# A graph attention layer's softmax by matrix products, its table in two parts, and layer 3 run from its last stage

## The chip, the core and the metric

The kernel runs on one core of a Trainium2 chip. The core has five engines, each with its own in-order queue: TensorE (PE; its weight loads are listed apart as PEld), VectorE (DVE), ScalarE (ACT), GpSimd (POOL) and SyncE (SP). SP issues most of the DMAs, POOL the indirect ones and some others. The metric is the time of one execution on the device in microseconds; three runs of the kernel before gave 2410.27, 2411.70 and 2413.79, a median of 2411.7.

## The reference

Four graph layers are applied in turn to x of shape 128 x 64 x 256 (graphs, nodes, features), each as `x = layernorm(x + layer(x))`. Layer 0 is a convolution with four windowed LSTMs, layer 1 a convolution with batch norms, layer 3 a spectral map with the eigenvectors U of the graph's Laplacian (`U (relu(U^T x W1 + b1) W2 + b2)`, per graph). Layer 2, which the change is about, is an attention over 512 edges `src -> dst` with 4 heads:

```
e     = a . leaky_relu(Xq[src] + Xq[dst])   + log(adj[src, dst] + eps)
m     = segment_max(e, src);  ex = exp(e - m[src])
attn  = ex / segment_sum(ex, src)[src]
Y     = segment_sum(attn * Xv[dst], src);   out = Y W_out^T
```

All is in float32.

## The kernel before

X (64 tiles of 128 rows by 256) stays in SBUF. The edges are sorted by source in layer 0 (`sort_edges`, lines 1396 to 1475), and per-edge tables are stored to DRAM as `edge_d` (line 1311) and loaded again for layer 2: `GG` (one-hot of source plus destination, both halves of the partitions), `lg` (logarithms), `kp` (1 where an edge has its predecessor's source), `br` (0 or -1e30 likewise) and `ix` (the row of the attention table for each edge). `attn_d` (line 1313) is that table in DRAM: 64 x 64 rows (destination, source) and 512 rows for edges that are not the last of their pair, 256 floats each; it is zeroed in layer 1 (line 1752).

Layer 2 has three kinds of steps, written as generators and run in an order written out by hand at the end of the kernel; the framework then orders instructions within each engine's queue, by their dependences, near that order.

- `scores` (lines 1908 to 1944), 32 steps of four tiles' worth of rows in two halves of 16 (HU). One step holds two half steps: 4 products with GG (line 1924), ACT's copies out of PSUM (1931), leaky ReLU on DVE (1932), and a half step later 4 products with `az` that sum over features (1878) into two PSUM tiles `sc`, one for each pair of heads. Between them stand the maps of the next step (1901), whose value part goes to DRAM (`xvd`, line 1905, issued by SP).
- the softmax of a half, when its 16 steps are through: `softmax` (1946 to 1964) adds `lg`, takes segment maxima by two scans on DVE, one forward and one backward, subtracts, takes exponentials on ACT, takes segment sums by two more scans, divides and multiplies, for two tiles of 128 x 512 each. `table` (1966 to 1979) transposes the result by PE, lets ACT scatter it into `at` (1974), and has POOL write it into `attn_d` with four indirect DMAs (1977). `fetch` (1981 to 1988) loads the table back as M with eight DMAs of 512 KB, all from SP, each row's 128 columns of 256.
- `values` (2014 to 2031), 33 steps: `load` copies one slice of M by ACT (`mc`, line 1993) and loads xv from DRAM by POOL's queue (1996), one step ahead; `mixed` multiplies (2008) and copies by ACT (`yT`, 2011); then the output product (2029), whose result `Norm` adds to X and normalises in groups of four tiles.

Layer 3 (`blocks`, 2127 to 2134) takes 16 blocks of four tiles through four stages, a software pipeline of 19 steps: `basis` (2096), after which POOL adds a constant `cb` to X (2100), `first_map` (2106), `back` (2114) and `second_map` (2123), with a last layer norm and the store of the block. Its weights are loaded (2066 to 2074) and its constants computed (2079 to 2084) after the scores.

The order: all scores of half 0; then scoring steps with the first softmax between them; table, fetch, scoring steps; seven pairs of scoring and value steps; then value steps, the second softmax and the first layer 3 steps mixed, the second table and fetch; then two value steps to one layer 3 step, and at the end the last layer 3 steps alone.

The functions that the change touches and what calls them:

Of the kernel before, what the change touches and what calls it, by code (L numbers as in the profile page):

```python
# [7 lines left out]
F32 = mybir.dt.float32  # L8
I32 = mybir.dt.int32
# [5 lines left out]
N = 64  # L15
# [1244 lines left out]
def tile_adj_resnorm(ctx: ExitStack, tc: tile.TileContext, I: dict, out: bass.AP, layers: int = 4):  # L1260
# [47 lines left out]
    EDGE = (("GG", E), ("lg", E), ("kp", E + 1), ("br", E + 1), ("ix", 4))  # L1308
# [4 lines left out]
    attn_d = dram.tile([N * N + E, 2 * P], F32, tag="attn_d", name="attn_d")  # L1313

    def edge_tables(t):
        at, o = 0, {}
        for name, w in EDGE:
            o[name] = t[:, at : at + w]
            at += w
        return [o[k] for k in ("GG", "lg", "kp", "br")] + [o["ix"].bitcast(I32)]  # L1320
# [75 lines left out]
    def sort_edges(gk, gp):  # L1396
# [5 lines left out]
        GG, lg, kp, br, ix = edge_tables(edge_s)  # L1402
# [54 lines left out]
        v.memset(kp, 0.0)  # L1457
        v.tensor_tensor(kp[:, 1:E], row[0][:, 1:], row[0][:, : E - 1], ALU.is_equal)
        v.tensor_scalar(br, kp, 1.0, 1e30, ALU.subtract, ALU.mult)
        OS, OD = gt_("kr", [P, E]), gt_("ef", [P, E])  # L1460
        v.tensor_scalar(OS, row[0], pmod, None, ALU.is_equal)
        v.tensor_scalar(OD, row[1], pmod, None, ALU.is_equal)
        v.tensor_tensor(GG, OS, OD, ALU.add)
        ps = gp.tile([P, 512], F32, tag="ps", name="ps")
# [287 lines left out]
    for z in attn_d[: N * N, :].rearrange("(k p a) q -> k p (a q)", p=P, a=4):  # L1752
        nc.sync.dma_start(z, zero)
# [73 lines left out]
    with ExitStack() as l2:  # L1827
# [9 lines left out]
        GG, lg, kp, br, ix = edge_tables(edge_s)  # L1837
# [16 lines left out]
        kf, kb, bf, bb = kp[:, :E], kp[:, 1:], br[:, :E], br[:, 1:]  # L1854
# [6 lines left out]
        es, soft = [[], []], []  # L1861
# [6 lines left out]
        def products():  # L1868
# [12 lines left out]
            if u_ == HU - 1 and c == 1:  # L1881
                next(soft[half])
# [63 lines left out]
        def softmax(half, es):  # L1946

            for c in range(2):
                es.append(sm.tile([P, E], F32, tag="se", name="se"))
                v.tensor_tensor(es[c], sc[half][c], lg, ALU.add)  # L1950
            yield
            for c, e in enumerate(es):
                f = sm.tile([P, 2, E], F32, tag="sf", name="sf", bufs=1)[:, 0, :]
                v.tensor_tensor_scan(f, bf, e, -1e30, ALU.add, ALU.max)
                v.tensor_tensor_scan(f[:, ::-1], bb[:, ::-1], f[:, ::-1], -1e30, ALU.add, ALU.max)
                v.tensor_tensor(e, e, f, ALU.subtract)
                s.activation(e, e, AF.Exp)
                yield
                v.tensor_tensor_scan(f, kf, e, 0.0, ALU.mult, ALU.add)
                v.tensor_tensor_scan(f[:, ::-1], kb[:, ::-1], f[:, ::-1], 0.0, ALU.mult, ALU.max)  # L1960
                yield
                v.reciprocal(f, f)  # L1962
                v.tensor_tensor(e, e, f, ALU.mult)
                yield

        def table(es):

            at = sm.tile([P, 2, E], F32, tag="sf", name="at", bufs=1).rearrange(
                "p a b -> p (a b)").rearrange("p (k b u c i) -> p k b u c i", k=4, b=2, u=HU, c=2)
            for c, e in enumerate(es):  # L1970
                ps = pp.tile([P, 512], F32, tag="m", name="m")
                for k in range(4):
                    te.transpose(ps[:, k * P : (k + 1) * P], e[:, k * P : (k + 1) * P], ident)
                s.copy(at[:, :, :, :, c, :].rearrange("p k b u i -> p (k b) i u"),
                       ps.rearrange("p (k i u) -> p k i u", i=4, u=HU))
            for k in range(4):
                nc.gpsimd.indirect_dma_start(
                    out=attn_d[:, :], out_offset=bass.IndirectOffsetOnAxis(ap=ix[:, k : k + 1], axis=0),
                    in_=at[:, k].rearrange("p b u c i -> p (b u c i)"), in_offset=None)

        def fetch(half):

            M2[half] = lw.tile([P, N, P], F32, tag="M2", name="M2", bufs=2)
            for n0 in range(0, N, 16):
                for b in range(2):
                    nc.sync.dma_start(  # L1986
                        M2[half][b * N : (b + 1) * N, n0 : n0 + 16, :],
                        attn_d[: N * N, b * P : (b + 1) * P].rearrange("(d n) q -> d n q", n=N)[:, n0 : n0 + 16, :])
# [25 lines left out]
        def values():  # L2014
# [3 lines left out]
            for k in range(K + 1):  # L2018
# [6 lines left out]
                if k:  # L2025
                    po = bank() if bank else pp.tile([P, 512], F32, tag="m", name="m")
# [10 lines left out]
        bank = None  # L2037
        sc_, beside[0] = scores(), last_pass()
# [4 lines left out]
        lw, sm = own1(valuing, name="l2w", bufs=1), own1(valuing, name="l2s", bufs=2)  # L2043
        ln = Norm(nc, sm, X, 4, act=True)
        val = values()
        soft += [softmax(h, es[h]) for h in range(2)]
        run(*[sc_] * (HU - NQ + 2))
        for _ in range(3):
            run(sc_, soft[0], soft[0])
        run(soft[0], sc_)  # L2050
        table(es[0])
        run(sc_)
        fetch(0)
        run(*[sc_] * 4)
# [6 lines left out]
        with tc.tile_pool(name="l3w", bufs=1) as l3w, tc.tile_pool(name="l3s", bufs=2) as s3, tc.tile_pool(  # L2061
            name="l3p", bufs=6, space=PSUM
        ) as p3:
            bank = lambda: p3.tile([P, 512], F32, tag="ps", name="ps")
            w1 = l3w.tile([P, 2, P], F32, tag="w31", name="w31")
            nc.sync.dma_start(w1, kio(I["W31"]))
            w2 = l3w.tile([P, D], F32, tag="w32", name="w32")
            nc.sync.dma_start(w2, I["W32"])
            b1 = l3w.tile([P, 1], F32, tag="b31", name="b31")
            nc.sync.dma_start(b1, I["b31"])  # L2070
            nb1 = l3w.tile([P, P], F32, tag="nb1", name="nb1")
            nc.sync.dma_start(nb1, I["b31"].rearrange("p o -> (p o)").partition_broadcast(P))
            cb = l3w.tile([P, D], F32, tag="cb", name="cb")
            nc.sync.dma_start(cb, I["b32"].partition_broadcast(P).rearrange("p o d -> p (o d)"))

            def constants():
                v.tensor_scalar(nb1, nb1, -1.0, None, ALU.mult)
                ps = bank()
                te.matmul(ps[:, :D], b1.to_broadcast([P, P]), w2, start=True, stop=True)
                te.matmul(ps[:, D : D + 1], bdut, ones[:, 0:1], start=True, stop=True)  # L2080
                ru = l3w.tile([P, 1], F32, tag="ru", name="ru")
                v.tensor_copy(ru, ps[:, D : D + 1])
                v.tensor_tensor(cb, cb, ps[:, :D], ALU.add)
                v.tensor_scalar(cb, cb, ru, None, ALU.mult)

# [32 lines left out]
            def second_map(q):  # L2118
                a = uh.pop(q)
                for j in range(0, 4, 2):  # L2120
# [4 lines left out]
                nc.sync.dma_start(ov[:, q * 4 : q * 4 + 4, :], X[:, q * 4 : q * 4 + 4, :])  # L2125

            def blocks():

                NQ = NT // 4
                for q in range(NQ + 3):  # L2130
                    for k, stage in enumerate((basis, first_map, back, second_map)):
# [5 lines left out]
            constants()  # L2137
            run(val, soft[1], val, soft[1], l3, soft[1], val, soft[1], l3, soft[1], val, soft[1], l3)
            table(es[1])
            run(val, l3)  # L2140
            fetch(1)
            run(*[val, val, l3] * 10)
            run(*[val] * 2, *[l3] * (NT // 4))
# [63 lines left out]
```

## Time and profile before

| | us |
|---|---|
| median of three runs | 2411.7 |
| the profiled execution | 2413.07 |
| its span | 2411.2 |
| layers 0 and 1 and the start of layer 2 (to about 1988) | 1988 |
| PE's wait at the first M (2071 to 2083) | 9.7 |
| PE's wait at the second M (2267 to 2276) | 9.4 |
| from PE's last matmul to the end | 12.3 |

The profile shows one execution. Each group of instructions is named by its line in the kernel before, its engine and `out<-in`. "Idle before" is the time in which the engine stood, with the instruction that ended it. A float32 product counts as two matmul records. The granted clock is the share of full speed that TensorE was given.

### The profile page before, as it was taken

What the parts mean: (1) busy time and instruction counts of PE and PEld (TensorE: products, weight loads), DVE (VectorE), ACT (ScalarE), POOL (GpSimd) and SP (SyncE); (2) the same over time, 40 slices, a digit from 0 to 9 for tenths busy, and PEclk for the clock granted to TensorE, in tenths of its full rate; (3) what the DMA queues carried; (4) which work ended last, traced back from release to release, by engine and by line L of the source; (5) the groups of instructions that cost most, each with busy time, mean ns of one, the idle gap of its engine ahead of it and who ended that gap; (6) DMA issues with size and microseconds to landing.
All of it is one profiled execution on the core that took longest, in us unless ns stands there. A gap on an engine that the chain in (4) does not pass through costs nothing. (4 is left out here: it accounts for less than half of the span.)

```text
span 2411.2 us, 29498 instructions
## 1 busy us (share of the span) xinstructions
PE 2289.0 (95%) x9016; PEld 1226.7 (51%) x9016; DVE 1815.5 (75%) x8352; ACT 974.3 (40%) x1750; POOL 76.4 (3%) x115
## 2 busy tenths in 40 slices
PE   7999999999999999999999999998979999898897
PEld 5544654444565544665444644554434433246786
DVE  4666766677887888888888888686967877457577
ACT  2333322242333243332243322333437875456575
POOL 0000000000000000000000000000000000002231
PEclk9999999999999999999999999999989999999899
DMA  6001000000100010100001000012211000511622
GB/s 218 18 18 36 1 35 1 24 30 18 53 1 35 2 52 18 53 35 1 35 36 36 17 18 18 18 49 92 75 45 40 23 23 29 94 40 44 136 89 75
DMA packets 59861, 101.26 MB, mean 42 GB/s; under 512 B 5136, under 2 KB 40080, under 8 KB 59440
## 3 DMA queue, kind: packets, MB, share of 16 engines
q1 hardware_dynamic: 54624, 88.83, 11.6%
q0 software_dynamic: 3216, 10.21, 1.5%
q8 instruction: 72, 1.18, 0.2%
q14 instruction: 93, 0.76, 0.1%
q10 hardware_dynamic: 1856, 0.28, 0.1%
HBM read 67.84 MB, written 31.46 MB: 41 GB/s over the span
## 5 line engine op out<-in xcount | busy, mean ns | idle before, releaser
L1590 PE MATMUL pq<-H,wi 128*128 128x512 f32 (+1 forms) x2016 | 836.4, 547 | 6.1 <-DVE H L1619 4.0
L1596 ACT ACTIVATE gate<-pq,bl 128x512 f32<-128x512 f32 (+1 forms) x504 | 317.6, 635 | 791.0 <-PE pq L1594 642.3
L1590 PEld LDWEIGHTS pq<-H,wi 128*128 128x128 f32 x2016 | 371.9, 191 | 331.0 <-issue 256.7
L1594 PE MATMUL pq<-lh,wh 128*128 128x512 f32 (+1 forms) x1152 | 481.8, 534 | 16.0 <-DVE lh L1614 12.7
L1594 PEld LDWEIGHTS pq<-lh,wh 128*128 128x128 f32 x1152 | 213.1, 190 | 213.3 <-issue 128.3
L1932 DVE SCALAR_TENSOR_TENSOR xs<-xs 128x512 f32<-128x512 f32 x256 | 165.3, 682 | 63.6 <-ACT xs L1931 62.5
L1931 ACT COPY xs<-l 128x512 f32<-128x512 f32 x256 | 136.8, 587 | 74.8 <-PE l L1924 38.6
L1924 PE MATMUL l<-edge_s,xq 64*128 64x512 f32 x512 | 136.0, 629 | 17.5 <-ACT xs L1931 12.5
L1612 ACT ACTIVATE gate<-lc 128x512 f32<-128x512 f32 (+1 forms) x144 | 83.5, 580 | 166.6 <-DVE lc L1608 80.9
L1901 PE MATMUL m<-wqv,xT 128*128 128x512 f32 x256 | 123.0, 617 | 0.8 <-DVE xT L1892 0.8
L1763 PE MATMUL ps<-h,w 128*128 128x512 f32 x256 | 114.9, 608 | 6.9 <-ACT h L1758 6.9
L1745 PE MATMUL ps<-at,w 128*128 128x512 f32 x256 | 116.7, 607 | 3.8 <-ACT at L1741 3.2
L1253 ACT ACTIVATE X<-X,ln_sh,ln_rs 128x256 f32<-128x256 f32 x192 | 99.2, 590 | 19.5 <-DVE ln_sh L1249 13.7
L1237 DVE BATCH_NORM_STATS2 ln_st<-X 128x6 f32<-128x256 f32 x256 | 98.7, 415 | 2.3
L142 DVE COPY AQR<-eps 64x192 f32<-64x192 f32 (+1 forms) x125 | 35.0, 280 | 80.9 <-PE eps L148 80.8
L1901 PEld LDWEIGHTS m<-wqv,xT 128*128 128x128 f32 x256 | 46.0, 192 | 77.1 <-issue 62.5
L1763 PEld LDWEIGHTS ps<-h,w 128*128 128x128 f32 x256 | 49.1, 194 | 67.4 <-issue 57.5
L1924 PEld LDWEIGHTS l<-edge_s,xq 64*128 64x128 f32 x512 | 46.3, 189 | 69.8 <-issue 32.9
L1996 POOL DMA_DIRECT2D xr<-xv x32 | 17.6, 550 | 2007.2 <-DVE xs L1932 1791.2
L1610 DVE TENSOR_TENSOR gate<-gate 128x512 f32<-128x512 f32 (+1 forms) x72 | 43.4, 603 | 45.9 <-ACT gate L1596 45.3
L1745 PEld LDWEIGHTS ps<-at,w 128*128 128x128 f32 x256 | 47.2, 192 | 59.7 <-issue 46.8
L1878 PE MATMUL sc<-xs,az 128*32 128x512 f32 x512 | 68.2, 605 | 3.0 <-DVE xs L1932 3.0
(557 smaller groups left out, 3245.6 us busy)
## 6 DMA issues: line engine op xcount, KB each, us to landing
wi<-in_WihT_dram SPq DMA_DIRECT2D x16, 1024.0 KB, 4.9
wh<-in_WhhT_dram SPq DMA_DIRECT2D x12, 1024.0 KB, 6.9
X<-in_x_dram SPq DMA_DIRECT2D x16, 512.0 KB, 8.9
xd<-X SPq DMA_DIRECT2D x16, 512.0 KB, 2.7
X<-xd SPq DMA_DIRECT2D x16, 512.0 KB, 3.2
xv<-xv SPq DMA_DIRECT2D x32, 256.0 KB, 2.0
xr<-xv POOLq DMA_DIRECT2D x32, 256.0 KB, 3.0
M<-attn_d SPq DMA_DIRECT2D x16, 512.0 KB, 11.2
```

The lines of the kernel that those rows point to most:

```text
L1237: nc.vector.bn_stats(st, self.X[:, k, :])
L1253: nc.scalar.activation(x, x, AF.Identity, bias=sh[:, k : k + 1], scale=rs[:, k : k + 1])
L1590: te.matmul(ps, wi[:, kk, o * P : (o + 1) * P], at(kk, k), start=(kk == 0), stop=(k == 0 and kk == 1))
L1594: te.matmul(ps, wh[:, kk, o * P : (o + 1) * P], hst[:, kk, :M], start=False, stop=(kk == 1))
L1596: s.activation(gates[gt][:, c, :M], ps, AF.Tanh if gt == 2 else AF.Sigmoid, bias=bl[:, p - 1, o : o + 1])
L1612: s.activation(g[2], cs, AF.Tanh)
L1745: te.matmul(ps, w1[:, k, c * P : (c + 1) * P], at[:, k, :], start=(k == 0), stop=(k == 1))
L1763: te.matmul(ps, w2[:, k, c * P : (c + 1) * P], h[:, k, :], start=(k == 0), stop=(k == 3))
L1901: te.matmul(ps, xT[:, i, c, :], wqv[:, c, :], start=(c == 0), stop=(c == 1))
L1924: mms.append(te.matmul(pl[i][:, b, :], xq[i][r, c * P : (c + 1) * P], GG[r, :], start=True, stop=True))
L1931: taken.append(s.copy(x, pl[i][:, b, :]))
L1932: ready.append(v.scalar_tensor_tensor(x, x, 0.2, x, ALU.mult, ALU.max))
```

## The change

The softmax's sums are no longer scans. Two tables are stored with the edges in place of `kp`: `OS`, the one-hot of each edge's source, and `OE`, its transpose in four parts (four PE transposes and one copy in `sort_edges`). After the exponentials the tile is transposed by PE and copied by ACT (`eT`); products with `OE` give the sums per source and row; their maximum with 0.5 is inverted on a 64 x 128 tile; products with `OS` spread the inverses over the edges; and DVE multiplies them with `eT` straight into `at`. `softmax` and `table` are one generator now. The second half's softmax takes each tile's maximum scan as soon as that tile's scores are complete, and stands between value steps alone, with no layer 3 step in it.

The attention table is two tables of 128 columns, so each half is written by four indirect DMAs of its own and read in contiguous runs; `fetch` takes one from SP and one from POOL.

Layer 3's weights and constants come during the scores. Two layer 3 steps stand before the second table's fetch and more right behind it, one to each value step. Within a layer 3 step the stages run from the last to the first. The last block is normalised and stored in two parts of two tiles.

```diff
-    EDGE = (("GG", E), ("lg", E), ("kp", E + 1), ("br", E + 1), ("ix", 4))
+    EDGE = (("GG", E), ("OS", E), ("lg", E), ("br", E + 1), ("OE", 4 * N), ("ix", 4))
...
-    attn_d = dram.tile([N * N + E, 2 * P], F32, tag="attn_d", name="attn_d")
+    attn_d = [dram.tile([N * N + E, P], F32, tag=f"attn_d{b}", name="attn_d") for b in range(2)]
...
+        ps = gp.tile([P, 512], F32, tag="ps", name="ps")
+        for k in range(4):
+            te.transpose(ps[:, k * N : (k + 1) * N], OS[:N, k * P : (k + 1) * P], ident[:N, :N])
+        v.tensor_copy(OE, ps[:, : 4 * N])
...
-    for z in attn_d[: N * N, :].rearrange("(k p a) q -> k p (a q)", p=P, a=4):
-        nc.sync.dma_start(z, zero)
+    for b in range(2):
+        for z in attn_d[b][: N * N, :].rearrange("(k p a) q -> k p (a q)", p=P, a=8):
+            nc.sync.dma_start(z, zero)
...
-            if u_ == HU - 1 and c == 1:
-                next(soft[half])
+            if u_ == HU - 1:
+                run(*[soft[half]] * (2 if half and not c else 1))
...
-        def softmax(half, es):
+        def softmax(half):
...
+            for f, c in ((scored, 0), (shifted, 0), (scored, 1), (shifted, 1)) if half else (
+                    (scored, 0), (scored, 1), (shifted, 0), (shifted, 1)):
+                f(c)
+                yield
+            for e in es:
                 s.activation(e, e, AF.Exp)
-                yield
-                v.tensor_tensor_scan(f, kf, e, 0.0, ALU.mult, ALU.add)
-                v.tensor_tensor_scan(f[:, ::-1], kb[:, ::-1], f[:, ::-1], 0.0, ALU.mult, ALU.max)
-                yield
-                v.reciprocal(f, f)
-                v.tensor_tensor(e, e, f, ALU.mult)
-                yield
+            yield
+            for e in es:
+                ps = scratch()
                 for k in range(4):
                     te.transpose(ps[:, k * P : (k + 1) * P], e[:, k * P : (k + 1) * P], ident)
-                s.copy(at[:, :, :, :, c, :].rearrange("p k b u i -> p (k b) i u"),
-                       ps.rearrange("p (k i u) -> p k i u", i=4, u=HU))
+                eTs.append(sm.tile([P, 4, P], F32, tag="sf", name="eT"))
+                s.copy(eTs[-1].rearrange("p k r -> p (k r)"), ps)
+            yield
+            for eT in eTs:
+                ps = scratch()
+                for k in range(4):
+                    te.matmul(ps[:N, :P], OE[:, k * N : (k + 1) * N], eT[:, k, :], start=(k == 0), stop=(k == 3))
+                rc = sm.tile([N, P], F32, tag="rc", name="rc")
+                v.tensor_scalar(rc, ps[:N, :P], 0.5, None, ALU.max)
+                v.reciprocal(rc, rc)
+                rcs.append(rc)
+            yield
...
+                for k in range(4):
+                    te.matmul(ps[:, k * P : (k + 1) * P], OS[:N, k * P : (k + 1) * P], rc, start=True, stop=True)
+                v.tensor_tensor(at[:, :, :, :, c, :].rearrange("p k b u i -> p (k b) i u"),
+                                eT.rearrange("p k (i u) -> p k i u", u=HU).rearrange("p k (b i) u -> p (k b) i u", b=2),
+                                ps.rearrange("p (k i u) -> p k i u", i=4, u=HU), ALU.mult)
             for k in range(4):
-                nc.gpsimd.indirect_dma_start(
-                    out=attn_d[:, :], out_offset=bass.IndirectOffsetOnAxis(ap=ix[:, k : k + 1], axis=0),
-                    in_=at[:, k].rearrange("p b u c i -> p (b u c i)"), in_offset=None)
+                for b in range(2):
+                    nc.gpsimd.indirect_dma_start(
+                        out=attn_d[b][:, :], out_offset=bass.IndirectOffsetOnAxis(ap=ix[:, k : k + 1], axis=0),
+                        in_=at[:, k, b].rearrange("p u c i -> p (u c i)"), in_offset=None)
...
-            M2[half] = lw.tile([P, N, P], F32, tag="M2", name="M2", bufs=2)
+            M2[half] = lw.tile([P, N, P], F32, tag="M2", name="M2")
             for n0 in range(0, N, 16):
                 for b in range(2):
-                    nc.sync.dma_start(
+                    (nc.sync, nc.gpsimd)[b].dma_start(
                         M2[half][b * N : (b + 1) * N, n0 : n0 + 16, :],
-                        attn_d[: N * N, b * P : (b + 1) * P].rearrange("(d n) q -> d n q", n=N)[:, n0 : n0 + 16, :])
+                        attn_d[b][: N * N, :].rearrange("(d n) q -> d n q", n=N)[:, n0 : n0 + 16, :])
...
-        for _ in range(3):
-            run(sc_, soft[0], soft[0])
-        run(soft[0], sc_)
-        table(es[0])
-        run(sc_)
+        run(*[sc_, soft[0]] * 6)
         fetch(0)
-        run(*[sc_] * 4)
+        run(*[sc_] * 3)
+        constants()
         run(*[sc_, val] * 7)
...
             def second_map(q):
                 a = uh.pop(q)
+                n = 4 if q < NT // 4 - 1 else 2
...
-                nc.sync.dma_start(ov[:, q * 4 : q * 4 + 4, :], X[:, q * 4 : q * 4 + 4, :])
+                    t = q * 4 + j + 2
+                    if t % n == 0:
+                        if n == 2:
+                            ln3.flush()
+                        nc.sync.dma_start(ov[:, t - n : t, :], X[:, t - n : t, :])
...
-                    for k, stage in enumerate((basis, first_map, back, second_map)):
+                    for k, stage in ((3, second_map), (2, back), (1, first_map), (0, basis)):
...
-            run(val, soft[1], val, soft[1], l3, soft[1], val, soft[1], l3, soft[1], val, soft[1], l3)
-            table(es[1])
-            run(val, l3)
+            run(sf, val, sf, val, sf, val, sf, val, sf, l3, l3, val, l3, val)
             fetch(1)
-            run(*[val, val, l3] * 10)
-            run(*[val] * 2, *[l3] * (NT // 4))
+            run(l3, val, l3, val, l3)
+            run(*[val, val, l3] * 8, val, val, *[l3] * (NT // 4))
```

`run` calls each generator it is given once, in order. `scratch` is a PSUM tile: of the pool that layers 2's products use before layer 3's pool is open, of that pool after.

## The prediction

> **What bounds the kernel.** I read the busy table first, then the stretches behind 1980 us, since every large edit is there, then who made TensorE wait, then the queues' timeline. Up to 1988 us PE is the bound and the change hardly touches it. The page's first line and five stretches (us; then busy time and instructions of PE, weight loads, DVE, ACT, POOL; granted clock, DMA share, GB/s):
>
> ```profile
> PE 2289.0 (95%) x9016; PEld 1226.7 (51%) x9016; DVE 1815.5 (75%) x8352; ACT 974.3 (40%) x1750; POOL 76.4 (3%) x115
> ```
> ```profile
> 1988.82:2041.01 52.19, 46.49 (x201) 16.24 (x201) 44.46 (x56) 27.09 (x57) 0.00 (x0) 0.97 0.07 26
> 2055.29:2080.07 24.78, 18.02 (x80) 6.25 (x72) 9.86 (x16) 8.39 (x19) 0.00 (x0) 0.92 1.12 188
> 2190.24:2290.97 100.73, 84.42 (x833) 72.76 (x829) 66.74 (x182) 60.76 (x115) 31.90 (x44) 0.88 0.46 100
> 2290.97:2398.87 107.90, 106.25 (x1024) 94.54 (x1024) 86.81 (x314) 74.42 (x160) 31.03 (x47) 1.00 0.24 77
> 2398.87:2411.20 12.33, 0.01 (x1) 0.00 (x0) 4.57 (x26) 6.31 (x14) 0.00 (x0) 0.70 0.38 128
> ```
>
> PE is full from 2291 to 2399 us, holed before that and idle at the end. In the second row the DMA engines are saturated (share 1.12). PE's waits from 2190 to 2280:
>
> ```profile
> PE m L2008 <- ACT mc L1993: 9.4, 1, 9.4
> PE m L1973 <- DVE se L1963: 3.4, 1, 3.4
> PE ps L2079 <- DVE is_t L1212: 2.3, 1, 2.3
> ```
>
> The first is the wait for the second table M, the second the softmax's division, the third the constants. The timeline around the first half's softmax and table, and the zeroing of the same 4 MB:
>
> ```profile
> 2002.81 3.35 DVE L1962 RECIPROCAL sf<-sf 128x512 f32<-128x512 f32 x1
> ```
> ```profile
> 2055.29 16.05 SPq L1986 DMA_DIRECT2D M<-attn_d  x8
> ```
> ```profile
> 1661.09 7.87 SPq L1753 DMA_DIRECT2D attn_d<-zero  x8
> 2276.40 3.26 PE L2008 MATMUL m<-mc,xr 64*64 64x64 f32 x64 [9.37 <-ACT mc L1993]
> ```
>
> The last line shows what an idle costs afterwards: 64 matmul records in 3.26 us, where undisturbed pairs of 32 take 1.8.
>
> **The change, part by part.** Times are on the clock of before.
>
> **A, first softmax among the scores.** A scoring step is 10.19 us undisturbed (two half steps of 5.1). From the matmuls at 1988.82 to those at 2036.88 stand 8 half steps, 40.8 us; 48.1 were spent, so the softmax cost 7.3, nearly all where DVE held the 3.35 us divisions and two more scans (1.21 each) per column tile in front of the leaky ReLUs. Its transposes cost another 1.0. Removed on DVE per half: 2 x (2 scans 2.4 + 3.35 + 0.68) = 12.9 us. Added on DVE: 2 x (a maximum on 64x128, by L2077 0.2; a division of 128 columns, 3.35/4 = 0.85, bounds 0.15 for four columns and 3.35; a product out of PSUM with scattered writes, 0.68 by L1950 to twice that, since ACT's scattered copy L1974 took 1.0 against 0.53 plain; I take 1.0) = 4.1. Added on PE: two groups of 8 products, each like L2106's 8 (1.79 us), 3.6 in all; bounds 2.0 (by the transposes' 1.0 for 8) and 4.5. PE is the bound here, so that counts in full. What DVE still delays I put at 1.4 (0 to 5): add, two scans and subtraction of the first tile cost 0.1 in the step from 1988.82 to 1999.12, the second tile's follow as closely. After: 1.0 + 3.6 + 1.4 = 6.0 against 8.3: **-2.3** (-5.3 to +2.5).
>
> **B, the wait for the first M.** Before, the transposes (2039.80) stand 5.5 half steps ahead of ACT's first copy out of M (queued in the 46th half step); M landed at 2080.07, PE stood 9.7 us and the step took 21.57 instead of 10.19: 11.4. In the changed order the sums stand after 42 half steps, the products after 44, and ACT's copies after 48. From the products PE has 30.0 us of work (their 1.8, then 5.5 half steps, matmuls of the 50th included) until it needs what lies behind those copies. The chain against it: product and DVE to the first scatter 3.5 (before 3.4); scatters: before 12.1 for four, 2.7 to 3.8 apart, of which POOL's issue is 1.0 and the rest a wait for the one before on the same table. Eight on two alternating tables fit the second issue into that wait, 13.1; bound above, no overlap, 8 x 2.7 = 21.6. Then M: rows of 512 bytes become runs of 8 KB; the nearest row is the zeroing, 4 MB in 4 KB runs, from 1661.09 to 4.9 us after its last issue at 1667.7, 11.5; I take 12, bounds 10 and the old 24.8. Then 3.0 from landing to PE, as at 2080.07 to 2083.10. Sum 31.6, so PE stands 1.6, with a slow stretch after it 2.6 of cost: **-8.8** (-11.4, no wait at all, to +4.6 with M at 24.8; the unoverlapped scatters alone make it -0.3).
> Here a rule speaks against the change: the Trainium skill, "DMA: Bandwidth & Descriptors", section "Issuing engines are not separate DMA queues", says that all queues end on the same 16 engines and a second one saves issue time alone. The saturated row agrees (share 1.12 while SP issued for only 16.05 of 24.78 us). By the rule alone, without the longer runs, M would take 24.8, PE would stand 14.4, and the sum below would be 13.4 us worse here and 5 in C; I follow the zeroing row instead.
> What is queued past: SP stands at M until the scatters are done, with one store of xv behind it (two buffers, so ACT is not held); layer 3's five loads (0.4 us of SP each) come up to the 13th scoring step, 2 us in all on SP, hidden by the scoring steps, whose stores come every 10 us; without that cover they cost their 2. POOL's xr loads wait behind the scatters and four M issues, and are needed only after M anyway.
>
> **C, second softmax, layer 3's start, second M.** From 2190.24 to 2290.97 the PE rows at undisturbed rates add up to 73.9 us (val step 2.73: 0.9 + 1.83; layer 3 block 6.19: 1.78 + 1.79 + 0.89 + 1.73), so 26.8 are waits and slow clock: 16.4 waits, the rest slow stretches such as 3.78 us for 8 products that take 1.79. After: 3.6 more products. The constants (0.8) move into the 51st half step; their 2.3 wait goes. The chain add, scans, subtraction, exponential, transposes, copy, sums, division, product is longer in links and still serial: by DVE's order the second tile's subtraction ends near 2205.5, its exponential 2206.4 (two table loads of 1.28 between), its copy on ACT, behind a layer norm's four (2.08) and another table load, 2212.8, sums 2213.7, products 2216.7 to 2218.5. PE's own work to there is 15.2 behind 2197.8, 2213.0: 5.5 wait, plus 1.5 slow clock. From there to the first matmul that needs the second M lie 42 us of PE work (val steps and layer 3 blocks). Scatters share POOL with eight additions of cb (0.75 each): products + 3.5 + 13 + 6 + landing 11 is about 34: no wait; bounds 0 and 5 (M as slow as before; 14 with scatters unoverlapped too). POOL's M issues stand behind an addition that waits for PE at products + 12.5, before the scatters are through; xr of val steps 15 and 16 stand behind them and are needed at + 39. DVE needs about 7.5 of the 8.9 us that a val step and a block take PE when they alternate one to one; for that coupling 2.0. After: 5.5 + 1.5 + 2.0 + 3.6 = 12.6 against 26.8: **-14.2** (-20 to 0).
>
> **D, the end.** Reversed stages expose the last copy of uh (about 1.1, as at L2123 before) but not two other stalls: 2.7 becomes 1.6. Behind PE's end 12.33 us stand: additions, statistics, eight normalisations in one run (4.02), store 4.4. With the last block normalised and stored in pairs, four remain behind the last statistics: 5.5 + 0.1 + 4.2 = 9.8. Together **-3.6** (-6 to 0).
>
> **E, the edge tables.** Four transposes, a 128x256 copy, 128 KB more to store and load once: **+0.5** (0 to +2). The zeroing has eight issues of 512 KB as before: 0.
>
> Sum: -2.3 - 8.8 - 14.2 - 3.6 + 0.5 = -28.4. The profiled execution took 2413.07 (span 2411.2 and 1.9 around it), 1.4 above the median: 2384.7 on its basis, 2383.3 on the median's. I say 2384.
>
> **Rivals.**
> 1. M is no faster (runs of 8 KB, or scatters that do not overlap). For: issue was not what limited it. Against: the zeroing row. B +13.4, C +5 (landing at 47 against 42): -10.0, 2402.
> 2. The second softmax's links starve PE: ACT's table loads and norms stand in front of each copy twice as long, and the clock falls. For: ACT's chain above already takes 6.4 us from the second exponential to its copy. Against: PE has val steps to fill with. If each link takes twice as long, C +12: -16.4, 2395.
> 3. Slower: POOL generates the four M issues per half so slowly that both M land late. For: SP needed 2.7 us for such an issue; against: POOL's xr issues of 128 rows took 0.55 and a scatter 1.0. At x us each, 4(x - 0.55) comes on B, and what exceeds 8 of it on C; that cancels 28.4 from x = 5.1 on; at 6 it is +7.2, 2419.
> 4. The products cost as much as the divisions did and waits only move: within 0.2% (4.8 us, about what a measurement of this kernel can tell from no change). Against: 3.6 of PE stands for 12.9 of DVE per half.
>
> **How the numbers follow.** Forecast 0.64, rival 1 0.14, rival 2 0.12, rival 3 0.07, rival 4 0.03; rivals 1 and 2 are faster too. Faster 0.90, same 0.03, slower 0.07. The terms' good ends (A -5, B -11, C -20, D -6) leave 2371 if all came together; I take 2372 to 2403, which takes in rivals 1 and 2 and leaves out rival 3.
>
> **What would show it.** A: no 128x512 reciprocal, the two groups of products near 1.8 us, steps behind the 32nd half step near 10.2 but for three of 11 to 12. B: M landing about 12 us after the last scatter, PE waiting under 4 us there. C: no wait for the second M, one hole of 5 us before the transposes. D: under 10 us behind the last matmul. Wrong if M's landings stay near 25 us, if POOL's M issues exceed 5 us, or if layer 3's blocks among the val steps stall.

## The result

The changed kernel takes 2421.9 us (2417.2 to 2426.3) against 2411.7: the ratio is 1.0038, interval 1.0020 to 1.0055. It is slower, by 0.4%, where 2384 was forecast and 2403 was the range's upper end. Its profiled execution is the fastest of its five: 2417.21 us, span 2415.4. Where its slower executions spend their 5 to 9 us more was not profiled; all that follows is about this one, 4.2 us longer in span than the profiled one of before.

Marks that both kernels have locate the difference. These are the X transposes that PE does for each scoring step (line 1890 before, 1896 after), the last product of the value steps (2029, 2055), and the end:

| mark | before, us | after, us | difference, us | gained or lost since the mark above |
|---|---|---|---|---|
| first transposes of the scores | 1807.18 | 1803.90 | -3.3 | -3.3 |
| 17th (before the first softmax) | 1978.01 | 1974.17 | -3.8 | -0.6 |
| 25th (softmax and products done) | 2067.83 | 2061.44 | -6.4 | -2.6 |
| 29th (M there, values begun) | 2120.98 | 2118.11 | -2.9 | +3.5 |
| last value product | 2372.87 | 2380.33 | +7.5 | +10.3 |
| end of the span | 2411.2 | 2415.4 | +4.2 | -3.3 |

The first 3.8 us say little of the change: in the twelve kernels below the first of these transposes began anywhere from 1803.1 to 1813.5 us, with all but the same work ahead of it.

The first line of the changed kernel's profile, then stretches that answer to those shown of before: the first softmax among the scores, the first M from its first issue to ACT's first copy, from the last scores to the first regular triple (two value steps and one layer 3 step), seven triples, and the end behind PE. The columns are as before: us, then busy time and instructions of PE, weight loads, DVE, ACT, POOL; granted clock, DMA share, GB/s.

```profile
PE 2292.2 (95%) x9084; PEld 1233.0 (51%) x9084; DVE 1798.8 (74%) x8355; ACT 969.7 (40%) x1751; POOL 86.3 (4%) x131
```
```profile
1984.98:2037.17 52.19, 50.63 (x223) 18.17 (x224) 36.20 (x53) 30.62 (x64) 0.00 (x0) 1.00 0.07 26
2068.53:2089.78 21.25, 13.42 (x58) 4.38 (x56) 5.86 (x9) 4.48 (x10) 2.15 (x4) 0.89 0.89 213
2187.37:2275.59 88.22, 80.12 (x788) 68.45 (x784) 58.31 (x177) 55.66 (x108) 33.04 (x48) 0.96 0.39 105
2275.59:2373.40 97.81, 85.66 (x883) 76.23 (x883) 60.84 (x225) 60.02 (x130) 25.28 (x40) 0.98 0.22 71
2407.18:2415.40 8.22, 0.00 (x0) 0.00 (x0) 3.38 (x20) 3.27 (x8) 0.00 (x0) 0.50 0.38 128
```

PE does 50.63 us of work in the softmax's stretch where it did 46.49, and the end behind PE is 8.22 us long and not 12.33: those parts do what was forecast. But M takes 21.25 us, and where PE used to be full it is busy for 85.66 of 97.81 us. PE's waits from the last scores on, and the timeline around the first M (SP, POOL, ACT, PE):

```profile
PE m L2034 <- ACT yT L2037: 17.7, 10, 3.5
PE ps L2148 <- ACT uh L2140: 2.9, 1, 2.9
PE ps L2055 <- ACT yT L2037: 2.3, 1, 2.3
```
```profile
2068.53 2.39 SPq L2012 DMA_DIRECT2D M<-attn_d  x4
...
2070.06 2.15 POOL L2012 DMA_DIRECT2D M<-attn_d  x4 [1.55 <-DMA attn_d<-at,edge_s]
...
2089.78 2.01 ACT L2019 COPY mc<-M 128x512 f32<-128x512 f32 x2 [13.46 <-DMA M<-attn_d]
...
2092.38 1.12 PE L1896 MATMUL m<-ident,X 128*128 128x128 f32 x4 [10.41 <-ACT xv L1910]
```

The wait for the second M that led the list of before (9.4 us at once) has given way to ten waits for `yT`. Seven of them are the 1.7 us of the regular triples below. The two longest, 3.55 and 1.82, come where the second M lands, when ACT's first copy out of it had waited 2.5 us. At the first M, ACT stands 13.46 us at its copy, and PE 10.41 us for a copy of `xv` that is queued behind that one on ACT.

A triple in the changed kernel, on PE and on ACT:

```profile
2289.56 0.98 PE L2034 MATMUL m<-mc,xr 64*64 64x64 f32 x32
...
2292.39 0.68 PE L2034 MATMUL m<-mc,xr 64*64 64x64 f32 x16
2294.81 0.68 PE L2034 MATMUL m<-mc,xr 64*64 64x64 f32 x16 [1.74 <-ACT yT L2037]
...
2303.54 0.98 PE L2034 MATMUL m<-mc,xr 64*64 64x64 f32 x32
```
```profile
2291.35 0.37 ACT L2037 COPY yT<-m 128x256 f32<-128x256 f32 x1
2292.43 2.08 ACT L1253 ACTIVATE X<-X,ln_sh,ln_rs 128x256 f32<-128x256 f32 x4 [0.71 <-DVE ln_sh L1249]
2294.41 0.35 ACT L2037 COPY yT<-m 128x256 f32<-128x256 f32 x1
```

From 2289.56 to 2303.54 it takes 13.98 us. Two triples of before, with PE busy throughout, took 11.85 each:

```profile
2303.13:2326.83 23.70, 23.70 (x258) 21.07 (x257) 18.54 (x67) 18.04 (x39) 7.75 (x12) 1.00 0.30 90
```

In the changed kernel PE stops in the middle of the second value step, because the second half of the first one's `yT` is still in PSUM: ACT has four normalisations in front of that copy, and before those a wait for DVE.

### The profile page after: what moved, and what is told of

The parts are those of the page before. It is cut to its first block, busy times and chain, and to the rows that moved or that the text cites. A ratio compares the mean times of both kernels' runs of the same rounds, so it can differ in the third digit from the quotient of the medians.

```text
span 2415.4 us, 29678 instructions
## 1 busy us (share of the span) xinstructions
PE 2292.2 (95%) x9084; PEld 1233.0 (51%) x9084; DVE 1798.8 (74%) x8355; ACT 969.7 (40%) x1751; POOL 86.3 (4%) x131
## 3 DMA queue, kind: packets, MB, share of 16 engines
q1 hardware_dynamic: 38640, 84.90, 10.1%
## 5 line engine op out<-in xcount | busy, mean ns | idle before, releaser
L1234 DVE TENSOR_TENSOR X<-ps,X 128x512 f32<-128x512 f32 x66 | 44.6, 675 | 46.4 <-PE ps L2055 44.1
```

## The experiments

The medians and the ratios to the kernel before, each timed beside it:

| run | us | ratio | interval |
|---|---|---|---|
| the change | 2421.9 | 1.0038 | 1.0020 to 1.0055 |
| x1 forward stages | 2403.9 | 0.9968 | 0.9957 to 0.9979 |
| x2 parity | 2418.5 | 1.0031 | 1.0021 to 1.0041 |
| x3 pitch | 2427.0 | 1.0060 | 1.0043 to 1.0077 |
| x4 wide DMAs | 2423.4 | 1.0043 | 1.0029 to 1.0057 |
| x5 one queue | 2414.2 | 1.0008 | 0.9998 to 1.0018 |
| x6 before, stages reversed | 2430.5 | 1.0068 | 1.0049 to 1.0087 |
| x7 five pairs | 2403.1 | 0.9962 | 0.9949 to 0.9974 |
| x8 three pairs | 2406.4 | 0.9975 | 0.9965 to 0.9984 |
| x9 ACT's copies held back | 2394.8 | 0.9921 | 0.9904 to 0.9939 |
| x10 the same, one queue | 2394.0 | 0.9921 | 0.9903 to 0.9938 |
| x11 the same, five pairs | 2387.1 | 0.9888 | 0.9871 to 0.9906 |
| x12 the same, drain reversed | 2384.1 | 0.9881 | 0.9863 to 0.9899 |

### What makes the triple longer

x1 turns the stages back:

```diff
-                    for k, stage in ((3, second_map), (2, back), (1, first_map), (0, basis)):
+                    for k, stage in ((0, basis), (1, first_map), (2, back), (3, second_map)):
```

> The changed kernel with one edit: within a layer 3 step the stages run from the first to the last again. In the changed kernel a triple (two value steps, one layer 3 step) takes 13.97 us, with PE waiting 1.74 us (by starts 1.97) before the second half of the second value step's products for ACT's copy of yT, which stands behind four normalisations; before it was 11.85 without such a wait. Theory A, the reversed stages put those normalisations in front of the copies: the triple goes back to about 11.9 us, the waits for yT fall from 17.7 us to under 5, and the time from about 2420 to 2403 to 2408 (eight triples at 2.0 less, some of it given back where the last stages drain). Theory B, it is not the order of the stages but which of the two value steps of a triple completes the group of four tiles that is normalised (the triples of before start at value step 12, those of the changed kernel at 15): the triple stays at 13.5 to 14.2 us and the time within 4 us of the changed kernel's.

x2 keeps them reversed and shifts the triples by one value step:

```diff
-            run(l3, val, l3, val, l3)
-            run(*[val, val, l3] * 8, val, val, *[l3] * (NT // 4))
+            run(l3, val, l3, val, val, l3)
+            run(*[val, val, l3] * 8, val, *[l3] * (NT // 4))
```

> The changed kernel with one edit: one value step is taken ahead of the triples, so that these start at value step 16, even as the 12 of before, and one stands behind them less. Theory A (the reversed stages make the wait): triples stay at 13.5 to 14.2 us, time within 4 us of the changed kernel's. Theory B (the parity of the value step at which a triple starts): the triple falls to about 11.9 us, the waits for yT from 17.7 us to under 6, the time to 2402 to 2408. If both have a share, the triple lies between, near 12.9.

x6 makes the reversal alone in the kernel before:

```diff
-                    for k, stage in enumerate((basis, first_map, back, second_map)):
+                    for k, stage in ((3, second_map), (2, back), (1, first_map), (0, basis)):
```

> The kernel before with one edit, the reversed order of the stages within a layer 3 step, and nothing else of the change. If the reversed order by itself makes ACT's copies of yT wait behind the normalisations: triples grow from 11.85 to about 14 us, ten of them stand in this kernel, and the time is 12 to 20 us longer than before, less 2 to 4 that the drain of the last stages gives back: 2420 to 2430. If the order costs only together with the rest of the change (the other count of value steps ahead of the triples, the stores in two parts), the triple stays at 11.9 and the time within 3 us of 2412.

Forward, the time is 2403.9, inside theory A's range. Two triples of that run, then ACT in one of them:

```profile
2278.68:2302.38 23.70, 23.70 (x257) 21.08 (x256) 19.14 (x66) 17.84 (x39) 7.75 (x12) 1.00 0.30 88
```
```profile
2291.32 0.65 ACT L2037 COPY yT<-m 128x256 f32<-128x256 f32 x2 [0.71 <-PE m L2034]
2291.86 1.09 ACT L2019 COPY mc<-M 128x512 f32<-128x512 f32 x1
2292.83 2.07 ACT L1253 ACTIVATE X<-X,ln_sh,ln_rs 128x256 f32<-128x256 f32 x4
```

Two triples in 23.70 us, PE busy in all of them: 11.85 each. Both halves of `yT` are copied ahead of the normalisations, and behind the scores the waits for `yT` on PE fall from 17.7 us to 0.2. The shift by one step (x2) leaves the triple at 13.85 (its first products at 2278.69 and 2292.54), so parity is not the cause; x2 has 14.2 us of waits for `yT` and 5.6 for an `xr` load. In the kernel before (x6) the reversal alone costs 17.6 us, and the same wait appears (PE):

```profile
2308.39 0.98 PE L2008 MATMUL m<-mc,xr 64*64 64x64 f32 x32
...
2313.23 0.97 PE L2008 MATMUL m<-mc,xr 64*64 64x64 f32 x32 [1.94 <-ACT yT L2011]
...
2322.25 0.97 PE L2008 MATMUL m<-mc,xr 64*64 64x64 f32 x32
```

13.86 from one triple to the next. So the reversed order costs 17 to 18 us in either kernel. The mechanism is read from ACT's rows, not varied by itself: with `second_map` first, layer 3's layer norm starts early in the step, its chain meets that of the value steps, and its four normalisations reach ACT ahead of a `yT` copy that holds a PSUM tile. In the profiled executions, from the 32nd transposes to the end, before takes 246.3 us, the change 253.4 and x1 236.3: the order costs 17.1, and the rest of parts C and D gains 10.1.

What is left in x1 is the second M. Its longest wait on PE, then POOL and ACT there:

```profile
PE ps L2148 <- DVE X L1234: 6.1, 1, 6.1
```
```profile
2242.68 2.15 POOL L2012 DMA_DIRECT2D M<-attn_d  x4 [6.33 <-DMA attn_d<-at,edge_s]
...
2257.87 1.05 ACT L2019 COPY mc<-M 128x512 f32<-128x512 f32 x1 [10.68 <-issue]
```

ACT stands 10.68 us at its first copy out of the second M. A short ACT step of the layer norm stands behind that copy, DVE waits for it, and PE waits for DVE. The rows suggest why M is late: with two tables SP could begin to read the first at 2233.71, and the last scatter into the second, issued 0.9 us later, landed only after 7.8 us instead of 2.2, so that POOL issued its half only at 2242.68. No run varies this by itself.

### Why M takes 21 us

x3 changes the distance between the 64 runs of a fetch, x4 makes one DMA reach all partitions (its scatters go to one table, with the indices of the second set of columns 64 x 72 rows higher). In both the rows' indices are worked out for 72 rows, and the zeroing covers the added rows. The main lines of x3, and below them of x4:

```diff
-    attn_d = [dram.tile([N * N + E, P], F32, tag=f"attn_d{b}", name="attn_d") for b in range(2)]
+    attn_d = [dram.tile([N * (N + 8), P], F32, tag=f"attn_d{b}", name="attn_d") for b in range(2)]
...
-                        attn_d[b][: N * N, :].rearrange("(d n) q -> d n q", n=N)[:, n0 : n0 + 16, :])
+                        attn_d[b].rearrange("(d n) q -> d n q", n=N + 8)[:, n0 : n0 + 16, :])
```

> The changed kernel with the table's rows laid out with 72 rows in place of 64 for each destination (the 8 added rows take the 512 rows of edges that are not the last of their pair), so that the 64 runs of 8 KB of a fetch lie 36 KB apart in DRAM and not 32 KB; two tables, two queues and 64 partitions for each DMA as in the changed kernel. In the changed kernel an 8 KB packet took about 640 ns where one queue worked alone and 490 where both did, 205 and 266 GB/s, against 159 ns for 4 KB packets elsewhere in the same execution (the loads of X, 128 partitions each). Theory P, the pitch of 32 KB makes the engines collide in DRAM: packets fall toward 320 ns, M lands 11 to 13 us after the first issue in place of 21, and the time falls by 8 to 14 us. Theory W, a DMA that reaches 64 of 128 partitions gets half the rate: packets stay at 600 to 650 ns where one queue works alone, M lands after 20 to 22 us, and the time stays within 3 us.

```diff
-                for b in range(2):
-                    (nc.sync, nc.gpsimd)[b].dma_start(
-                        M2[half][b * N : (b + 1) * N, n0 : n0 + 16, :],
-                        attn_d[b][: N * N, :].rearrange("(d n) q -> d n q", n=N)[:, n0 : n0 + 16, :])
+                x = nc.sync.dma_start(M2[half][:, n0 : n0 + 16, :],
+                                      attn_d.rearrange("(p n) q -> p n q", n=N + 8)[:, n0 : n0 + 16, :])
...
```

> The changed kernel with both tables in one piece of DRAM, 72 rows for each destination as in the run with the other pitch, so that one DMA of 1 MB brings 16 rows for all 128 partitions; M comes in four of these, all from SP. Scatters go to the one table, and their order among themselves is left free as it is between the two tables. Theory W (a DMA into 64 partitions gets half the rate): 8 KB packets fall to 310 to 350 ns, M lands 11 to 13 us after the last scatter in place of 21 to 22, PE's wait at the first M falls from 10.4 us to under 2, the wait behind the second M goes, and the time falls by 12 to 18 us, to about 2403 to 2408. Theory P (the pitch) gives the same here, and is told apart by the run with the pitch alone. If neither, and all 16 engines are simply full at about 200 GB/s on reads from this table, M stays at 20 to 22 us.

x5 leaves the table as it is and has one queue:

```diff
-                    (nc.sync, nc.gpsimd)[b].dma_start(
+                    nc.sync.dma_start(
```

> The changed kernel with one edit: all eight DMAs of a fetch are issued by SP, none by POOL. In the changed kernel the first packets of POOL's queue moved about 5 us after its first issue, and its last part was moved by that queue alone. Theory W (a DMA into 64 partitions gets half the rate, about 205 GB/s, and only while DMAs for both halves are in flight from two queues is it more, 266): one queue takes 4.2 MB / 0.205 = 20.5 us plus 2 to 3 of latency, M lands 22 to 24 us after the first issue in place of 21.2, and the time is 0 to 6 us longer than the changed kernel's. If the second queue was worth what its share of the bytes suggests, M would take 30 us or more and the time would grow by 15. If POOL's issue was a drag, M lands sooner than 21 us and the time falls by 2 to 6.

The stretch from the first M issue to ACT's first copy in x3, then x4, then x5; the changed kernel's is the second row of its stretches above:

```profile
2078.72:2099.64 20.92, 12.85 (x56) 4.22 (x48) 5.45 (x9) 3.92 (x10) 2.15 (x4) 0.89 0.89 216
```
```profile
2083.08:2095.95 12.87, 7.63 (x38) 2.92 (x30) 2.67 (x5) 1.72 (x5) 0.00 (x0) 1.00 0.91 349
```
```profile
2073.20:2095.16 21.96, 18.83 (x84) 6.85 (x76) 10.51 (x18) 8.44 (x19) 0.00 (x0) 1.00 0.95 218
```

The pitch changes nothing (20.92 us). DMAs that reach all 128 partitions bring the same 4 MB in 12.87. The share is 0.9 in all of them, the rate 349 against 213 to 218 GB/s: the engines are as busy, each with slower packets. In the middle of x4's fetch:

```profile
2086.50:2091.50 5.00, 4.23 (x22) 1.44 (x18) 0.25 (x1) 0.00 (x0) 0.00 (x0) 1.00 1.00 424
```

x4's DMAs are also larger, 1 MB and not 512 KB. That alone is not the cause: the loads of X at the start, 512 KB each over 128 partitions, land 1.5 us apart in the changed kernel, about 350 GB/s. The Trainium skill has the rule, "SBUF — State Buffer", section "Door 1: The DMA port swizzle": partitions 0 to 63 reach 8 of the 16 ports that DMAs enter by, 64 to 127 the others, so a transfer into one half has half the rate (the page: about 218 of 436 GB/s). These runs agree, with 206 and 424 GB/s. Within the changed kernel's fetch, where SP's queue worked alone, and where both did:

```profile
2072.50:2075.00 2.50, 2.50 (x16) 0.59 (x14) 1.41 (x3) 1.07 (x2) 0.00 (x0) 1.00 1.03 206
2077.50:2083.00 5.50, 4.47 (x20) 1.22 (x16) 0.00 (x0) 0.00 (x0) 0.00 (x0) 1.00 1.00 265
```

So the second queue, which brings the other half, adds 59 GB/s while both are busy (29%), and over a whole fetch it gains 0.7 us (21.25 against 21.96). The same page says under "Can I just issue two DMAs to hit both halves?" that such a pair gains 6%; while both queues are full it is more here, over the fetch less.

The forecasts of time failed. x3 was to stay within 3 us of the change and is 5.0 longer by the medians; but in its profiled execution the scores began 9.6 us later than in the changed kernel's, and from there to the end the two differ by less than 0.5. x4 was to be 12 to 18 us faster and is not faster at all: its scatters were not left free as that text has it: with one table each waits for the one before it, and eight took 22.0 us to the first M issue (2061.03 to 2083.08) where two tables took 11.1 (2057.42 to 2068.53), so that M landed no sooner. And x5 was to be slower, but is 7.7 us faster than the change. What moved is not M but ACT: its first copy out of M stands after 49.5 half steps in the order of x5, after 48 in the changed kernel. From the 26th to the 28th transposes x5 takes 27.6 us, the changed kernel 35.3.

### What sets the wait at the first M

x7 and x8 (both forward) move value steps from the scores to behind the second fetch. x7 is shown; x8 has 7, 3 and `val, val, l3` three times.

```diff
-        run(*[sc_] * 3)
+        run(*[sc_] * 5)
         constants()
-        run(*[sc_, val] * 7)
+        run(*[sc_, val] * 5)
...
-            run(l3, val, l3, val, l3)
+            run(l3, val, val, l3, val, val, l3)
```

> The changed kernel with the stages forward, as in the first run, and two value steps moved from the scores to behind the second fetch: five scoring steps stand alone after the first fetch instead of three, then five pairs instead of seven, and two more value steps stand between the second fetch and the step that needs the second M. If M's landing is all that holds PE there: the wait of 10.5 us at the first M and the 3 us of slow clock behind it go (20 us more of scores cover it), the wait of 6.1 at the second falls to under 2 (5.5 us more of products cover it), and the time is 2380 to 2390 against the 2404 of the forward run. If something else is late there (the xr loads, the softmax's chain, ACT's copies), the waits only change their names and the time stays above 2396.

> As the run before, but four value steps are moved: seven scoring steps stand alone, then three pairs, and behind the second fetch four more value steps than in the changed kernel. If cover for M is what counts and the run before has enough of it at the first M: nothing more is won there, the second wait goes altogether, and pairs that cost 14.2 us against 10.2 + 2.7 for the two apart save 1.3 each: 2376 to 2386, 2 to 6 below the run before. If value steps beside the scores are the cheaper place, it is slower than the run before by 2 or more.

The gains failed to come: x7 is 0.8 us faster than x1, x8 2.5 slower. That is the other branch of x7's text: something else is late there. x8 is 3.3 slower than x7, as its own other branch has it, but its wait for `xr` below would make that by itself. PE's longest two waits of x7 behind the first softmax, and ACT at its first M:

```profile
PE m L1896 <- ACT xv L1910: 11.5, 1, 11.5
PE m L2034 <- DMA xr<-xv: 8.4, 1, 8.4
```
```profile
2094.32 2.00 ACT L2019 COPY mc<-M 128x512 f32<-128x512 f32 x2 [14.51 <-DMA M<-attn_d]
```

ACT waits for M about as long as in x1 (13.59 us). In the order of both runs its first two copies stand after 48 half steps still: the value steps were written later, but nothing tied these copies to them, and the framework put them where it did before. Why there, no profile tells. The second wait (14.6 us in x8) is for an `xr` load that POOL issued right behind its half of M. In the changed kernel such a load took up to 14.2 us to land, with a median of 2.9. In the kernel before, with all of M from SP, the longest took 10.2.

x9 takes x1 and ties these copies behind the last copy of scores written ahead of them, which puts the first two after 52 half steps (`after` with `NoSync` orders an instruction behind others without a wait; `newest` holds the last copy of scores):

```diff
+                        newest[:] = taken[-1:]
...
-            s.copy(m.rearrange("p c i h n -> p (c i h) n"),
-                   M2[half][:, :, u_ * 8 : u_ * 8 + 8].rearrange("p n q -> p q n"))
+            after(s.copy(m.rearrange("p c i h n -> p (c i h) n"),
+                         M2[half][:, :, u_ * 8 : u_ * 8 + 8].rearrange("p n q -> p q n")),
+                  newest, mybir.DependencyClass.NoSync)
```

> The forward run with one addition: ACT's copies out of M are kept, by an order without a wait, behind the last copy of scores that was written ahead of them. In the changed kernel, and in the runs with five and with three pairs alike, the first two of these copies stand on ACT after 48 half steps, wherever the value steps were written; with one queue they stood at 49.5 and 50. Here they stand after 52. Theory Q, ACT's place in its queue decides: M (20 to 22 us after the last scatter, near 2090 when the scores begin at 1811) lands before ACT reaches the copies (near 2097), the wait of 10.5 us and the slow clock of 3 us behind it go, nothing is late in its place, and the time is 2388 to 2393 against the forward run's 2404. Theory M, it is M's landing that decides wherever the copies stand: then the wait moves to the products that need them, and the time stays within 4 us of 2404.

x10 is x9 with one queue (the edit of x5):

> The run before (forward, ACT's copies kept behind the scores) with all of M's DMAs from SP. In the five-pair run PE waited 8.4 us for an xr load, which POOL issues: its packets stand behind POOL's share of M. If that queue behind M is a cost of its own, the second M's stretch gets no longer with one queue although M lands 1 to 3 us later: 2385 to 2393, at most 2 above the run before. If the second queue was worth its while, this is 3 to 8 us slower than the run before.

ACT's first copies out of M in x9:

```profile
2100.11 2.09 ACT L2020 COPY mc<-M 128x512 f32<-128x512 f32 x2
```

In x9 the copies start without a wait and PE's 10.5 us are gone. That is worth 9.1 us by the medians (2403.9 to 2394.8), not 11 to 16: the step with the first value step now takes 16.4 us against 10.2 for a plain one, with rows in it at about half speed (eight matmul records of line 1884 in 1.93 us, otherwise 1.07). With one queue (x10) it is the same time, and no product waits for `xr`. But its `xr` loads are not early: one that POOL issued at 2239.0, while M came in from SP, moved nothing before 2245 and its last packets by 2250, 11 us after the issue. So it is not POOL's half of M alone that makes these loads late. The second queue is thus worth nothing here. Over the whole kernel that agrees with the rule that the prediction weighed and set aside, that queues end on the same engines.

### A version that beats both

x11 joins what held: forward stages, ACT's copies tied, one queue, five pairs. x12 is x11 with the stages reversed where no value step runs beside them (the line is shown against that of the change):

```diff
-                    for k, stage in ((3, second_map), (2, back), (1, first_map), (0, basis)):
+                    for k, stage in ((0, basis), (1, first_map), (2, back), (3, second_map))[:: 1 if q < 14 else -1]:
```

> Forward stages, ACT's copies kept behind the scores, all of M from SP, and five pairs instead of seven (two value steps moved behind the second fetch, as in the five-pair run). If the five-pair run failed only because ACT's first copies stayed in place and xr stood behind M: no wait at the first M, under 3 us at the second, and 2376 to 2384. If the second M still holds ACT or PE for 6 us or more, it is 2385 or more.

> The run before with the stages reversed in layer 3's last five steps alone, when no value step runs beside them. From the last value product to the end the kernel before took 38.3 us, the changed one 35.1 and the forward run 36.9, so the reversed order is worth 1.8 us there and the last block in two parts about 1.4: 1 to 3 us below the run before. If the reversed order gains nothing by itself, it is within 1 us of it.

x11 takes 2387.1: with ACT's copies tied and no product waiting for `xr`, the two moved value steps are worth 6.9 us, less than forecast; ACT still stood 8.2 us at the second M. x12 takes 2384.1, 2.9 less by the medians, though their times overlap; in the profiled executions it gains 1.9 from the last value product to the end, where 1.8 was expected of the order. PE's longest waits behind its scores are these:

```profile
PE m L2036 <- ACT yT L2039: 4.5, 3, 2.5
PE ps L2150 <- ACT uh L2142: 2.9, 1, 2.9
PE ps L2057 <- ACT ag L2124: 1.5, 1, 1.5
```

It is 1.2% faster than before (ratio 0.9881) and, by the medians, 37.8 us faster than the change as it was made.

## Why the prediction was wrong

The sum gave -28.4 us; the profiled executions differ by +4.2. By its terms:

- **A, first softmax:** -2.3 forecast, -2.6 measured (the upper bound is +2.2 by its own terms, not +2.5). Its parts hold too: a division on 64 x 128 took 0.87 us (0.85 assumed), the scattered product 1.0 (1.0), sums and products on PE 3.8 (3.6).
- **B, first M:** -8.8 forecast; +3.5 measured, with 0.7 of constants that C had counted. The steps up to the fetch were right or better: scatters 11.1 us (13.1 assumed). The term that failed is "I take 12" for M. The row it came from, the zeroing, writes to DRAM from all 128 partitions; M's DMAs read into 64. The row of M itself, 24.8 us, was the near one: same direction, same partitions. It was measured at 21.25, close to the bound that was kept for the range; longer runs and a second queue bought 3.5 us, of which 2.8 stay with one queue (x5). The reading of that row as engines at their limit, by its share of 1.12, was wrong too: it moved 188 GB/s, and x4 moves 424 at a share of 1.00. PE's cover was as forecast (28.8 us, 30.0 assumed), so PE stood 10.4 us where 1.6 was said, with a slow stretch behind it. The second thing missed: the cover was taken as given, but x9 shows that it depends on where ACT's copies stand.
- **C, second softmax, layer 3, second M:** -14.2 forecast, +10.3 measured up to the last value product. The step that failed is "for that coupling 2.0", and behind it the assumption that triples stay at 11.85 whatever the order of stages. DVE's load was counted, ACT's queue was not. No term was given to the order there. With the stages forward (x1) the part gains 8.6, so the order made 18.9 of the 24.5 us of miss (it gave 1.8 back in D: 17.1 up to the end). In the other 5.6 the second M is the larger item, forecast at no wait: x1 waited 6.1 us at it and ran about 2.9 us of products slower behind it. Here too "landing 11" was the mis-sized term: the second M took 21.8 us in the changed kernel and 23.9 in x1. Against that the softmax's own waits on PE were 1.8 us, where 5.5 were said.
- **D, the end:** -3.6 forecast, -3.3 measured. The number came out by luck, its parts did not: behind PE's end 4.1 us were gained where 2.5 were said, and from the last value product to PE's end 0.8 were lost where 1.1 were to be gained; the exposed copy of `uh` alone is a wait of 2.85 there. And of the two causes named the split of the last block alone does not shorten what stands behind PE: in x1, with the split and forward stages, 12.45 us stand behind PE, as before. With reversed stages and no split (x6) it is 10.1, with both 8.2.
- **E:** +0.5 forecast; not to be told from the 3.8 us by which the scores began earlier.

C and D together miss 24.9 us, B 12.3; A and the start give 4.6 back; that makes the 32.6.

Of the rivals, the first came nearly true in its condition (M no faster; it took 21.25 of the 24.8 us) and would have given 2402; its own cost is in B and C. The rest, 17 us, was in no rival. The second asked whether ACT's norms stand in front of copies, in the wrong place: at the softmax, where the change adds links, and not in the regular triples, where it only reorders. The third is refuted, POOL's four M issues took 2.15 us. Of the signs of being wrong, "if layer 3's blocks among the val steps stall" named the failure, without a price.

## What to carry to other kernels

Price a transfer by a row that has its direction and its partitions: 64 partitions and 128 differ by more here than runs of 512 bytes and of 8 KB. Where steps are reordered, write out every in-order queue for one period, ACT's too, and ask which short copy that frees a buffer now stands behind long work; a triple that was full says nothing on the next order. And when a wait is to be covered by moved work, look first where the waiting instruction itself stands in its engine's queue: moving the work around it may not move it.

## What the runs showed of the hardware

- DMAs into 64 partitions moved 206 GB/s, with both halves in flight from two queues 265, and DMAs over all 128 partitions 424; 4 MB took 21.25 us by the first kind on two queues and 12.87 by the last. The busy share of the DMA engines is 1.0 in each of the three, so a full share does not mean full rate.
- Runs 32 KB or 36 KB apart in DRAM made no difference (21.25 and 20.92 us).
- A load issued while M comes in can land late, whichever queue M is on: an `xr` load took 2.9 us by the median, up to 14.2 with half of M on POOL's own queue (the change), up to 10.2 (before) and about 11 (x10) with all of M on SP's.
- A scatter issued 0.9 us after M's first read landed after 7.8 us instead of 2.2 (x1).
- Scatters to two tables followed each other by 1.3 to 1.7 us, to one table by 2.5 to 3.4.
